# Two GNN layers on one core: PSUM banks shared by all uses, results taken seven chunks after their products

## The chip, the core and the metric

The kernel runs on one core of one Trainium2 chip. The metric is the device time of a run in microseconds (us). Three runs of the kernel before gave 1674.48, 1678.09 and 1674.82 us.

## What is computed

A graph network of two GIN layers, then a residual and a layer norm, all in float32. There are 6250 nodes with 256 features and 100000 edges, sorted by destination. Low-numbered nodes have many more edges than high-numbered ones.

```python
def agg(h, eps): return (1 + eps) * h + segment_sum(h[src], dst, 6250)
h = agg(x, eps1)                       # 6250 x 256
h = relu(h @ W1a + b1a)                # 256 -> 512
h = relu(h @ W1b + b1b)                # 512 -> 512
h = agg(h, eps2)                       # 6250 x 512
h = relu(h @ W2a + b2a)                # 512 -> 512
out = layernorm(x + (h @ W2b + b2b))   # 512 -> 256, no scale or shift
```

## The kernel before

The nodes are 49 tiles of 128 rows, and the edges 782 chunks of 128. Both layers run the same function, `layer`, which writes out the order of every engine's work by hand: a Python loop issues instructions, and each engine executes its own in that order.

**Edges that are counted.** The destinations of the first 216 chunks all lie in the four "heavy" tiles 0 to 3. For these, layer 1 makes a table of how often each source meets each destination (`counting`): per step DVE makes two one-hot tables (ca, cb; `make`), TensorE multiplies them into PSUM (pc, L775), ACT copies the result (cs, L766), DVE adds it to the table at (L750). The table, converted to float32 and multiplied with the features (`products`: pm<-xr,cf, L683; 13 ranges of four source tiles for each of four heavy tiles), gives the sums of the heavy tiles; DVE adds each of the 52 results to the accumulator acc (L689). Layer 1 stores the table in HBM (counts, SP queue, L759) and layer 2 loads it from there (L696).

**Edges that are gathered.** The other 566 chunks are 94 groups of 20 down to 4 chunks (63 have 4). GpSimd issues an indirect DMA for each chunk (`gather`, L264) that brings the 128 source rows into a ring of 24 chunks: 6 pieces of 4, each refilled when TensorE has used it. Layer 1 keeps the ring in early; layer 2, whose rows are twice as wide, in early and late. In the main loop each piece of four chunks is summed by TensorE against one-hot tables sel (pm, L887, 32 columns a chunk, four chunks beside each other). When a group is complete, ACT copies the sum (split<-pm, L906), TensorE moves its rows to their places (pu<-split,to, L911), and DVE adds it to the accumulators of the three or four tiles it may belong to, under a mask (L915). DVE makes sel and to of the group after next right after a group (`select`, L552, L557).

**Dense layers.** Accumulators are held for blocks of four tiles, at most four blocks at a time (ACCS). `seed` loads a block's own rows into acc (SP queue, L535), and five chunks later ACT multiplies them by 1 + eps (L542), for which it waits until they have landed. When all groups and products of a block are added, `block` runs the two dense layers: transposes (pt, L611; copied by ACT to zt, L614), first matrix (ph, L623; ACT's relu to ht, L627), second matrix (po, L634), then `finish` (layer 1: DVE add, ACT relu, store of h on ACT's queue; layer 2: DVE adds and statistics, and in `conclude2` the norm and the store on SP's queue, L991).

**The order.** Three things are woven together in the main loop. After each chunk, `now` goes up by one, `due` issues what was put off with `later`, and two queues are pumped: blockwise (the dense layers, a credit of up to 4.0 us) and beside (counting and products), at a rate that `spread` plans. Each step yields its planned TensorE cost. Of the blocks only the first in the queue advances.

**PSUM.** There are eight banks of 512 float32 columns. In layer 1 three hold sums (pm, pu and products; `sum_tile`), three the dense results (mm) and two the counts (pc); in layer 2 five hold sums and three dense results. A sum is taken LAG = 2 chunks after it was asked for, or when its bank is needed; pu follows split by one chunk. Dense results are copied right after their product (zt, ht), or one chunk after (`finish`).

## Time and profile before

| | |
|---|---|
| median of three runs | 1674.82 us |
| the profiled execution, its own time | 2010.4 us |
| its span, first to last instruction | 2008.7 us |
| mean granted TensorE clock | 0.853 |
| busy: TensorE, DVE, ACT, GpSimd | 1405.2, 822.3, 371.4, 1087.8 us |
| idle time of GpSimd that a wait for pm (L887) ended, both layers | 309.4 us |
| adds of products to acc (L689) | 104, 57.7 us |

The profile is of one execution, which was longer than the three runs. In a group of instructions the page gives busy time, the mean of one and the idle time before them with what ended it. "Remote", and in the chain of waits "another core or an unknown queue", means that the profile shows no event that ended a wait. Each float32 matmul has two records.

### The profile page before, as it was taken

What the parts mean: (1) busy time and instruction counts of PE and PEld (TensorE: products, weight loads), DVE (VectorE), ACT (ScalarE), POOL (GpSimd) and SP (SyncE); (2) the same over time, 40 slices, a digit from 0 to 9 for tenths busy, and PEclk for the clock granted to TensorE, in tenths of its full rate; (3) what the DMA queues carried; (4) which work ended last, traced back from release to release, by engine and by line L of the source; (5) the groups of instructions that cost most, each with busy time, mean ns of one, the idle gap of its engine ahead of it and who ended that gap; (6) DMA issues with size and microseconds to landing.
All of it is one profiled execution on the core that took longest, in us unless ns stands there. A gap on an engine that the chain in (4) does not pass through costs nothing.

```text
span 2008.7 us, 17209 instructions
## 1 busy us (share of the span) xinstructions
PE 1405.2 (70%) x5364; PEld 617.0 (31%) x5364; DVE 822.3 (41%) x2256; ACT 371.4 (18%) x683; POOL 1087.8 (54%) x1147
## 2 busy tenths in 40 slices
PE   1344757674867887978656858695869768878877
PEld 0111223332433444423312223241323323324334
DVE  4665453534344434333111213332425355456543
ACT  0222232321322222212100001111101111112111
POOL 5666665656556556451276755656555464455520
PEclk9766787787878988988878879797979889989989
DMA  5433354546436557331487766757676475565631
GB/s 150 139 92 92 97 176 144 169 144 180 149 119 205 172 174 224 116 110 48 175 290 241 242 203 212 228 178 234 192 234 199 126 261 161 154 193 173 180 102 38
DMA packets 157811, 337.08 MB, mean 168 GB/s; under 512 B 23954, under 2 KB 70930, under 8 KB 157712
## 3 DMA queue, kind: packets, MB, share of 16 engines
q0 software_dynamic: 72448, 222.63, 37.0%
q1 hardware_dynamic: 74756, 96.90, 14.4%
q10 hardware_dynamic: 10508, 16.35, 2.3%
q8 instruction: 47, 0.77, 0.2%
q14 instruction: 52, 0.43, 0.1%
HBM read 303.75 MB, written 32.05 MB: 167 GB/s over the span
## 4 chain that ended last, share of the span: by engine, by line
PE 41%; issue 18%; another core or an unknown queue 15%; DVE 11%; DMA 6%; POOL 4%; ACT 3%; SPq 1%; DVEq 0%; ACTq 0%; POOLq 0%
PE ph L623 12%; PE po L634 10%; PE pm L683 8%; PE pm L887 5%; PE pu L911 4%; POOL early L264 3%; DVE acc L915 3%; DMA acc<-h 2%; DVE at L750 1%; PE pc L775 1%; PE pt L611 1%; ACT split L906 1%; ACT zt L614 1%; DVE cb L736 1%
## 5 line engine op out<-in xcount | busy, mean ns | idle before, releaser
L264 POOL DMA_INDIRECT early<-in_x_dram,srcs x566 | 547.0, 967 | 366.4 <-issue 149.2
L264 POOL DMA_INDIRECT early<-h,srcs x288 | 274.1, 952 | 267.9 <-PE pm L887 84.2
L915 DVE SCALAR_TENSOR_TENSOR acc<-pu,mask,acc 128x256 f32<-128x256 f32 (+1 forms) x666 | 365.2, 608 | 105.6 <-PE ph L623 22.9
L264 POOL DMA_INDIRECT late<-h,srcs x278 | 263.4, 948 | 210.6 <-PE pm L887 109.4
L683 PE MATMUL pm<-xr,cf 128*128 128x256 f32 (+3 forms) x784 | 311.0, 545 | 44.8 <-issue 21.1
L911 PE MATMUL pu<-split,to 128*128 128x256 f32 (+2 forms) x376 | 186.8, 583 | 206.1 <-ACT split L906 136.8
L689 DVE TENSOR_TENSOR acc<-pm,acc 128x256 f32<-128x256 f32 (+1 forms) x104 | 57.7, 556 | 415.5 <-remote 162.5
L683 PEld LDWEIGHTS pm<-xr,cf 128*128 128x128 f32 (+1 forms) x784 | 165.4, 218 | 202.5 <-issue 152.0
L887 PE MATMUL pm<-early,sel 128*32 128x256 f32 (+1 forms) x1708 | 191.4, 527 | 49.6 <-issue 16.5
L623 PE MATMUL ph<-zt,w2a_s 128*128 128x512 f32 (+1 forms) x416 | 184.9, 596 | 27.8 <-ACT zt L614 27.7
L775 PE MATMUL pc<-cb,ca 128*128 128x490 f16 x216 | 87.7, 475 | 141.5 <-issue 41.6
L634 PE MATMUL po<-w1b_s,ht 128*128 128x512 f32 (+1 forms) x392 | 175.5, 599 | 0.0
L911 PEld LDWEIGHTS pu<-split,to 128*128 128x128 f32 (+1 forms) x376 | 70.6, 215 | 304.6 <-ACT split L906 174.4
L906 ACT COPY split<-pm 128x256 f32<-128x256 f32 (+2 forms) x188 | 88.0, 479 | 362.6 <-remote 164.6
L766 ACT CAST cs<-pc 128x490 f16<-128x490 f32 x151 | 84.0, 570 | 199.7 <-remote 115.6
L623 PEld LDWEIGHTS ph<-zt,w2a_s 128*128 128x128 f32 x416 | 78.5, 199 | 136.6 <-issue 89.5
L552 DVE TENSOR_TENSOR sel<-iota,slot 128x128 f32<-128x128 f32 (+5 forms) x188 | 65.4, 348 | 124.0 <-remote 96.7
L623 PE MATMUL ph<-zt,w1a_s 128*128 128x512 f32 (+1 forms) x208 | 102.3, 629 | 7.7 <-issue 5.1
L887 PE MATMUL pm<-late,sel 128*32 128x512 f32 x556 | 90.0, 647 | 18.1 <-issue 14.4
L557 DVE TENSOR_SCALAR to<-iota,home 128x128 f32<-128x128 f32 x188 | 57.4, 305 | 109.5 <-PE pu L911 66.9
L634 PEld LDWEIGHTS po<-w1b_s,ht 128*128 128x128 f32 (+1 forms) x392 | 74.1, 191 | 89.0 <-issue 87.1
L614 ACT COPY zt<-pt 128x256 f32<-128x256 f32 (+2 forms) x98 | 44.7, 483 | 284.1 <-remote 209.3
(111 smaller groups left out, 941.2 us busy)
## 6 DMA issues: line engine op xcount, KB each, us to landing
xr<-in_x_dram SPq DMA_DIRECT2D x48, 512.0 KB
h<-h1r ACTq DMA_DIRECT2D x48, 256.0 KB
counts<-cf SPq DMA_DIRECT2D x48, 256.0 KB
acc<-h SPq DMA_DIRECT2D x12, 1024.0 KB
xr<-h SPq DMA_DIRECT2D x12, 1024.0 KB
cf<-counts SPq DMA_DIRECT2D x48, 256.0 KB
early<-in_x_dram,srcs POOLq DMA_INDIRECT x566
acc<-in_x_dram SPq DMA_DIRECT2D x12, 512.0 KB
```

The lines of the kernel that those rows point to most:

```text
L264: nc.gpsimd.indirect_dma_start(out=rows_[:, j, :], out_offset=None, in_=table, in_offset=bass.IndirectOffsetOnAxis(ap=srcs[:, c : c + 1], ...
L552: nc.vector.tensor_tensor(sel[:, :n, :], iota[:, :SLOTS].unsqueeze(1).to_broadcast([P, n, SLOTS]), slot[:, c0 : c0 + n].unsqueeze(2).to_br ...
L614: nc.scalar.copy(zt[:, :, i * P : i * P + m], pt[:, :, :m])
L623: nc.tensor.matmul(ph[:, :nb], wa[:, k, f * P : (f + 1) * P], zt[:, k, :nb], start=(k == 0), stop=(k == kk - 1),)
L634: nc.tensor.matmul(po[:m], ht[:, f, i * P : i * P + m], wb[:, f, :], start=(f == 0), stop=(f == KH - 1),)
L683: nc.tensor.matmul(pm, cf[:m, j, :], xr[:m, j, :], start=(j == 0), stop=(j == len(ks) - 1),)
L766: nc.scalar.copy(cs, pc)
L775: mm = nc.tensor.matmul(pc, a, b, start=(i == 0), stop=(i == len(pair) - 1))
L887: mm = nc.tensor.matmul(pm[b * SLOTS : (b + 1) * SLOTS], sel[:, c - c0, :], rows_[:, j, :], start=(c == parts[b][0]), stop=(c == parts[b][ ...
L906: nc.scalar.copy(split[:used], pm[:used])
L911: nc.tensor.matmul(pu, to[:used], split[:used], start=True, stop=True)
L915: nc.vector.scalar_tensor_tensor(acc[t], pu, mask[:, t - lo[g], g : g + 1], acc[t], op0=ALU.mult, op1=ALU.add,)
```

## The change

`sum_tile`, `take` and the three PSUM pools go. Each layer holds eight bank tiles, in 16 halves, and `place(n)` gives a half (up to 256 columns) or a whole bank to any use: pm, pu, products, pc, pt, ph, po. Halves whose neighbour is in use go first. While an accumulation of several matmuls is open, nothing else is put in its bank. When nothing is free, the result that is due first is taken at once. LAG is 7 for all of them, and now for zt, ht, `finish` and cs too; pu follows split by two chunks, and the add to the table follows cs by two.

A block counts its results that are still to be taken (pending), and yields None while there are any; the blockwise queue has two hands and then lets the next block take a step. In layer 1 the 13 products of a heavy tile stay open in one bank (`once`) and are added once. The products of a heavy tile start when its counts have been added. The order of `select` moves: half a group later, for groups of over 4 chunks. There are more buffers for sel of small groups (4), to (6), split (3) and cs (4). Set-up tables that only the preparation uses are moved to its pool; the clearing of dsti goes from GpSimd to DVE. The core of the diff, with removed lines left out from `later` on:

```diff
@@ -27,7 +27,10 @@
 STEP1 = 1.1
 STEP2 = 1.5
 ACCS = 4
-LAG = 2
+LAG = 7
+BLOCKS = 2
+BANKS = 8
+BANK = 512
 SPREAD = 5.0
 TILES = 4
 SIGMAS = 6.5
...
@@ -504,9 +507,12 @@
             edge = ctx.enter_context(tc.tile_pool(name=f"edge{number}", bufs=3))
             dense = ctx.enter_context(tc.tile_pool(name=f"dense{number}", bufs=2))
             psum = ctx.enter_context(
-                tc.tile_pool(name=f"psum{number}", bufs=2, space=bass.MemoryType.PSUM)
+                tc.tile_pool(name=f"psum{number}", bufs=1, space=bass.MemoryType.PSUM)
             )
-            SUMS = 3 if number == 1 else 5
+            banks = [
+                psum.tile([P, BANK], F32, tag=f"bank{i}", name=f"bank{i}") for i in range(BANKS)
+            ]
+            halves = [(i, j) for i in range(BANKS) for j in range(2)]
             acc = {}
             held = []
...
             def seed(ts):
                 while len(held) >= ACCS:
+                    if not blockwise.todo:
+                        due(all=True)
                     assert blockwise.todo
                     blockwise.step()
+                    tick()
                 held.append(ts)
                 a = edge.tile([P, TILES, width], F32, tag="acc", name="acc", bufs=ACCS)
...
@@ -562,39 +578,70 @@
             delayed = []
             now = 0
...
+            def later(chunks, what, frees=False):
+                delayed.append((now + chunks, what, frees))
+            def undelay(item):
+                delayed.remove(item)
+                item[1]()
             def due(all=False):
                 while delayed:
                     item = min(delayed, key=lambda d: d[0])
                     if not all and item[0] > now:
                         break
...
+                    undelay(item)
                 for b in list(waiting):
                     if not any(uses[t] or left[t] for t in b):
                         blockwise.todo.append(block(b))
                         waiting.remove(b)
...
+            def tick():
+                nonlocal now
+                now += 1
+                due()
+            opened = []
+            def place(n, whole=False):
+                while True:
+                    here = [h for h in halves if h[0] not in opened]
+                    single = [h for h in here if (h[0], 1 - h[1]) not in halves]
+                    double = [h for h in here if (h[0], 1 - h[1]) in halves]
+                    if 2 * n <= BANK and (single or double):
+                        i, j = (single or double)[0]
+                        mine = [(i, j)]
+                        break
+                    if 2 * n > BANK and double:
+                        i = next(h[0] for k, h in enumerate(double) if (h[0], 1 - h[1]) in double[:k])
+                        j = 0
+                        mine = [(i, 0), (i, 1)]
+                        break
+                    undelay(min((d for d in delayed if d[2]), key=lambda d: d[0]))
+                for h in mine:
+                    halves.remove(h)
+                if not whole:
+                    opened.append(i)
+                return banks[i][:, j * BANK // 2 : j * BANK // 2 + n], mine
+            def complete(p):
+                opened.remove(p[1][0][0])
+            def free(p):
+                halves.extend(p[1])
+            def take_later(p, what):
+                def take():
+                    what(p[0])
+                    free(p)
+                later(LAG, take, frees=True)
@@ -602,44 +649,66 @@
                 nb = sum(rows(t) for t in ts)
                 early = prepare(dense, ts)
+                pending = 0
+                def result(p, what):
+                    nonlocal pending
+                    def taken():
+                        nonlocal pending
+                        pending -= 1
+                    def take(ap):
+                        what(ap)
+                        later(1, taken)
+                    pending += 1
+                    take_later(p, take)
                 zt = dense.tile([P, kk, TILES * P], F32, tag="zt", name="zt")
                 for i, t in enumerate(ts):
                     m = rows(t)
...
+                    pt = place(kk * P, whole=True)
                     a = acc.pop(t)
                     for k in range(kk):
                         nc.tensor.transpose(
...
+                            pt[0][:, k * P : k * P + m], a[:m, k * P : (k + 1) * P], ident[:m, :m]
                         )
...
+                    result(pt, lambda ap, i=i, m=m: nc.scalar.copy(
+                        zt[:, :, i * P : i * P + m],
+                        ap.rearrange("p (k j) -> p k j", j=P)[:, :, :m],
+                    ))
                     if t == ts[-1]:
                         held.remove(ts)
                     yield 0.11 * kk
...
+                while pending:
+                    yield None
                 ht = dense.tile([P, KH, TILES * P], F32, tag="ht", name="ht")
                 for f in range(KH):
...
+                    ph = place(TILES * P, whole=True)
                     for k in range(kk):
                         nc.tensor.matmul(
...
+                            ph[0][:, :nb], wa[:, k, f * P : (f + 1) * P], zt[:, k, :nb],
                             start=(k == 0), stop=(k == kk - 1),
                         )
...
+                    result(ph, lambda ap, f=f: nc.scalar.activation(
+                        ht[:, f, :nb], ap[:, :nb], AF.Relu, bias=ba[:, f : f + 1]
+                    ))
                     yield 0.00167 * kk * nb
...
+                while pending:
+                    yield None
                 for i, t in enumerate(ts):
                     m = rows(t)
...
+                    po = place(wide, whole=True)
                     for f in range(KH):
                         nc.tensor.matmul(
...
+                            po[0][:m], ht[:, f, i * P : i * P + m], wb[:, f, :],
                             start=(f == 0), stop=(f == KH - 1),
                         )
...
+                    result(po, lambda ap, t=t, m=m, i=i: finish(dense, t, m, ap, i, early))
                     yield 0.00167 * KH * wide
...
+                while pending:
+                    yield None
                 yield from conclude(dense, ts, early)
             def products(turns, table_of):
@@ -676,20 +745,24 @@
                         load(i + 1)
                     xr, cf = factors.pop(0)
                     ks = ranges[r]
...
+                    opens = not once or r == 0
+                    closes = not once or r == len(ranges) - 1
+                    if opens:
+                        pm = place(width)
                     for j, k in enumerate(ks):
...
+                            pm[0], cf[:m, j, :], xr[:m, j, :],
+                            start=(opens and j == 0), stop=(closes and j == len(ks) - 1),
                         )
...
+                    def add_product(ap, t=t):
+                        nc.vector.tensor_tensor(acc[t], ap, acc[t], op=ALU.add)
                         left[t] -= 1
...
+                    if closes:
+                        complete(pm)
+                        take_later(pm, add_product)
                     yield 0.00167 * len(ks) * width
             def load_counts(cf, r, ks, t):
...
@@ -760,29 +833,30 @@
                         counts[r, t, :, : n * P], cf[:, :n, :].rearrange("p k j -> p (k j)")
                     )
...
                 def step():
                     c, pair, made = ready.pop(0)
...
+                    pc = place(NT * W, whole=True)
                     for i, (a, b) in enumerate(pair):
                         mm = nc.tensor.matmul(
...
+                            pc[0], a, b, start=(i == 0), stop=(i == len(pair) - 1)
                         )
                         if i == 0:
                             together(mm, [made])
...
+                    def copy(ap, c=c):
+                        cs = edge.tile([P, NT * W], F16, tag="cs", name="cs", bufs=4)
+                        nc.scalar.copy(cs, ap)
+                        later(2, lambda: add(c, cs))
+                    take_later(pc, copy)
                     if todo:
                         make(*todo.pop(0))
                     return STEP1 if len(pair) == 1 else STEP2
+                def products_of(t):
+                    while added <= end[t]:
+                        yield 0.0
+                    yield from products([(r, t) for r in range(len(ranges))], convert)
                 total = len(todo)
                 make(*todo.pop(0))
...
@@ -796,39 +870,40 @@
                 for t in heavy:
                     n = end[t] + 1 - steps
+                    d = min(LAG + 3, n // 2)
                     for i in range(n):
                         steps += 1
                         yield step()
...
+                        if i >= d:
+                            k = len(ranges) + 1
+                            for _ in range((i + 1 - d) * k // (n - d) - (i - d) * k // (n - d)):
+                                yield next(product, 0.0)
                     yield from product
...
+                    product = products_of(t)
                 yield from product
...
             class Queue:
...
+                def __init__(self, rate, hands=1):
                     self.rate = rate
                     self.credit = 0.0
                     self.todo = []
+                    self.hands = hands
+                    self.over = []
                 def step(self):
...
+                    for w in self.todo[: self.hands]:
+                        if w not in self.over:
+                            cost = next(w, self)
+                            if cost is self:
+                                self.over.append(w)
+                            elif cost is not None:
+                                self.credit -= cost
+                                break
+                    while self.todo and self.todo[0] in self.over:
+                        self.over.remove(self.todo.pop(0))
                 def pump(self):
                     self.credit = min(self.credit + self.rate, 4.0)
...
@@ -844,7 +919,7 @@
             due(all=True)
             select(order[0])
             select(order[1])
...
@@ -893,44 +967,44 @@
                     last_sum[upto] = mm
                     gathered[upto + PIECES] = gather(upto + PIECES, table, width, *places)
                     for c, b in pieces[upto][1]:
...
+                        tick()
                         for q in both:
                             q.pump()
                     upto += 1
...
+                def add_group(ap, g=g, to=to, parts=parts):
+                    split = edge.tile([P, width], F32, tag="split", name="split", bufs=3)
                     used = SLOTS * sum(1 for p in parts if p)
...
+                    nc.scalar.copy(split[:used], ap[:used])
+                    def add(ap):
+                        for t in range(lo[g], min(hi[g], NT - 1) + 1):
+                            nc.vector.scalar_tensor_tensor(
+                                acc[t], ap, mask[:, t - lo[g], g : g + 1], acc[t],
+                                op0=ALU.mult, op1=ALU.add,
+                            )
+                            uses[t] -= 1
                     def unite():
...
+                        pu = place(width, whole=True)
+                        nc.tensor.matmul(
+                            pu[0], to[:used], split[:used], start=True, stop=True
+                        )
+                        take_later(pu, add)
+                    later(2, unite)
+                complete(pm)
+                take_later(pm, add_group)
                 if k + 2 < len(order):
...
+                    n = len(members[order[k + 1]])
+                    later(n // 2 if n > PARTS else 0, lambda k=k: select(order[k + 2]))
             due(all=True)
             blockwise.todo += [block(b) for b in waiting]
             while blockwise.todo:
                 blockwise.step()
...
+                tick()
             due(all=True)
         def prepare1(dense, ts):
```

## The prediction, made before the changed kernel was run

> **What bounds the kernel now.** I read the page first, then the busy time by stage, then the timeline across one long stall, then TensorE's waits.
>
> ```profile
> PE 1405.2 (70%) x5364; PEld 617.0 (31%) x5364; DVE 822.3 (41%) x2256; ACT 371.4 (18%) x683; POOL 1087.8 (54%) x1147
> ...
> PE 41%; issue 18%; another core or an unknown queue 15%; DVE 11%; DMA 6%; POOL 4%; ACT 3%; SPq 1%; DVEq 0%; ACTq 0%; POOLq 0%
> ...
> L264 POOL DMA_INDIRECT early<-in_x_dram,srcs x566 | 547.0, 967 | 366.4 <-issue 149.2
> ```
>
> No engine is full. The chain that ended last spends 15% of 2008.7 us, 307 us, on a releaser that the profile can't name. I cut the span where the gathers of each layer begin to follow TensorE and where they end:
>
> ```profile
> core 0: us, PE busy (x) PEld busy (x) DVE busy (x) ACT busy (x) POOL busy (x), PEclk, DMA share, GB/s
> 0.00:54.00 54.00, 10.81 (x46) 5.44 (x50) 26.77 (x216) 0.00 (x0) 27.27 (x40) 1.00 0.49 148
> 54.00:917.00 863.00, 582.59 (x2445) 272.64 (x2438) 387.09 (x1174) 217.55 (x431) 522.67 (x542) 0.82 0.48 146
> 917.00:987.00 70.00, 53.31 (x167) 23.61 (x165) 16.70 (x39) 16.41 (x31) 0.79 (x2) 0.92 0.15 52
> 987.00:1933.00 946.00, 699.70 (x2481) 283.39 (x2482) 358.95 (x749) 124.23 (x195) 536.72 (x566) 0.87 0.66 208
> 1933.00:2009.00 76.00, 58.78 (x236) 31.95 (x234) 32.76 (x80) 13.23 (x27) 0.31 (x1) 0.96 0.10 32
> ```
>
> The columns are microseconds with counts in brackets, then the granted clock. The two long stages hold 1809 of 2009 us. TensorE is idle in 26 to 32% of them, and its clock is down to 0.82 and 0.87. Now one stall in layer 2:
>
> ```profile
> 1042.80 1.18 PE L887 MATMUL pm<-late,sel 128*32 128x512 f32 x8 [2.34 <-DMA late<-h,srcs]
> ...
> 1058.95 0.94 POOL L264 DMA_INDIRECT early<-h,srcs  x1 [0.30 <-issue]
> 1063.61 0.58 ACT L906 COPY split<-pm 128x512 f32<-128x512 f32 x1 [40.91 <-remote]
> 1063.61 0.69 DVE L552 TENSOR_TENSOR sel<-iota,slot 128x512 f32<-128x512 f32 x1 [18.22 <-remote]
> 1063.85 1.27 POOL L264 DMA_INDIRECT early<-h,srcs  x1 [3.96 <-remote]
> ```
>
> All engines stand still while GpSimd works off its gathers, 1.25 us apart, and all start together. The chain's unnamed part is 18.8% of the layer 1 stage (162 us) and 15.2% of the layer 2 stage (144 us).
>
> ```profile
> PE pu L911 <- ACT split L906: 136.8, 42, 20.3
> ...
> PE pc L775 <- ACT cs L766: 33.9, 10, 14.6
> ...
> PE ph L623 <- ACT zt L614: 30.3, 7, 15.0
> PE pc L775 <- DVE ca L732: 29.4, 11, 6.8
> ...
> PE pt L611 <- ACT zt L614: 27.6, 4, 7.8
> ```
>
> These are microseconds, times and the longest. They are the waits the change can reach: TensorE waits for a PSUM result to be copied (split, zt, cs) before it uses the copy or the bank.
>
> **The profiled time and the median.** The profiled execution took 2010.4 us (span 2008.7), the shown runs 1674.82 in the median: 336 less. The unnamed 307 us nearly close that gap (2010 - 307 = 1703), so I take them to belong to the profiled execution and count them neither as a gain nor as a loss. Without them the stages are 54 + 701 + 70 + 802 + 76 = 1703, which is 28 above the median.
>
> [...] clock 0.65 in 100-200 us with TensorE 46% busy, 0.97 in 1800-1900 us at 91%. [...] So I use the spacing of gathers, not their record of 0.95 us.
>
> **The floor.** Gathers that don't wait are 1.25 us apart (1057.69, 1058.95 and so on; 0.95 of record and 0.30 of issue). Layer 1 needs 542 x 1.25 = 678 us in its stage, layer 2 566 x 1.25 = 708. TensorE's own work at full clock, from undisturbed runs of the chain (0.429 us a 512-wide record, half for 256, 3.06 us for 24 gather records): in layer 2, ph 416 x 0.429 = 178, products 392 x 0.429 = 168, pm 1132 x 0.1275 = 144, po 392 x 0.216 = 85, pu 188 x 0.429 = 81, pt about 22: 678 us. In layer 1 the same sum is about 511 (po 168, ph 89, products 84, pm 74, pc 45, pu 40, pt 11). So GpSimd's spacing is the floor in both: room is 701 - 678 = 23 us in layer 1 and 802 - 708 = 94 in layer 2, 117 in all. Less the 28 that the median already lacks: **89 us of room**, floor 1675 - 89 = 1586.
>
> **The change, part by part.**
> 1. LAG 2 to 7, unite 1 to 2 chunks. A copy or add now enters the ACT or DVE queue about 7 x 1.25 = 8.8 us after its product rather than 2.5, and pu waits two chunks for split. Nothing is added to run; work is moved later in two queues. What it removes: pu for split 136.8, pc for cs 33.9. Much of that lies inside the unnamed stalls (20.28 us of it in the one shown), so it isn't all a gain.
> 2. Eight shared banks. Without them LAG 7 would run out. Demand in layer 2, a group of 4 chunks: pm (4 + 7)/4 = 2.75, pu 7/4 = 1.75, products 52 x 7/566 = 0.64, a block of 12 results each 40 chunks or so 12 x 7/40 = 2.1: 7.2 of 8. When none is free the oldest result is taken early; the real lag then is some 4 to 6 chunks. Cost between 0 and 1 us a time; I take 0, because that result is ready by then.
> 3. Two blocks at a time; a phase waits for its copies by letting other work pass. Removes ph for zt 30.3 and pt for zt 27.6 (again partly inside stalls). A block now takes about 12 steps and three pauses of 8 chunks, 36 chunks, just within the 36 to 40 at which blocks come, so no extra block is left for the end. If one were, about 22 us would follow a layer's last gather. I take 0. What moves with a result moves whole: in layer 1 the DVE add, ACT's relu and the store of h on ACT's queue; in layer 2 four DVE instructions, and by the longer pauses the store of the output, which sits on SP's queue ahead of later counts and seed loads. That queue waited 386 us for the output's rows already (L991), while nobody waited much for counts (11.2 us), so I price the move at 0 to 10 us and take 0.
> 4. Layer 1's products stay open over 13 ranges: 52 adds of about 0.42 us become 4. That is 20 us less on DVE, which is 45% busy there: 0 on the path.
> 5. sel is issued up to half a group later, with 4 buffers for small groups: bound -3 to +3 us; I take 0.
> 6. The seeds' loads and the ACT scale behind them (ACT acc for DMA acc<-h, 71.9 us in 7 waits, longest 30.4) stay. ACT still stops there; what is queued behind it is split and zt. TensorE now has 9 us of slack before it needs them. Accumulators are held 11 chunks longer; by the schedule at most four are held, so seeds keep their lead.
> 7. Set-up memsets moved; dsti's 0.75 us goes from POOL to DVE: under 1 us, hidden by loads.
>
> **What is late next** is the gather. TensorE must keep 1.25 us a chunk; at full clock layer 2 asks 678/566 = 1.20. At a clock of 0.94 they are equal, and it has 0.87 now. Hence not all of the room: of the 89 I take layer 1's share whole (23 x 89/117 = 17) and two thirds of layer 2's 72, 48: 65. **Forecast 1675 - 65 = 1610 us**, its own range 1588 to 1640.
>
> **Rivals.**
> - *The gather spacing isn't the floor in unprofiled runs.* For it: TensorE nearly never waits for gathers (7.9 + 2.3 + 5.2 us). Against: the spacing is so constant. Then the gain is the named waits outside the unnamed stalls: the TensorE waits of both stages that parts 1 to 3 reach sum to 299 us; the unnamed 307 of 526 us idle are 58%, leaving 42%, 126: **1549**.
> - *Slower: halves of one bank serialise.* In layer 1 pm, pu and pt take halves, and a half whose neighbour is unread is preferred. If a read must wait for the newest write beside it, and TensorE for the read, each of 188 results costs a round trip: pm's end to pu through split was about 1.2 us (at 1022). TensorE's 583 busy us reach 701 with 98 of these; that is where it decides. With three quarters (141 x 1.2 = 169) layer 1 is at 752, 51 worse; with 20 gained in layer 2, **1706**. Against: pieces of 4 chunks are written at once, and the oldest free half is taken first.
> - *Little:* the waits go over to the acc<-h loads and to SP's queue, which the change leaves; only 5 to 10 us are won: **1668**.
>
> **Chances.** Forecast 0.60; gathers not the floor 0.14; little 0.13; slower 0.13. About 0.2% is what a measurement can tell from no change here. Faster 0.60 + 0.14 + 0.08 = 0.82, same 0.05, slower 0.13. The range holds the forecast's case, most of the first rival's and of the third: 1545 to 1670.
>
> **What would show it.** Right: pu for split, pc for cs, ph and pt for zt nearly gone; clock over 0.9 in both long stages; gathers that wait for pm (115.8 us in layer 1, 193.6 in layer 2) at a third; TensorE waiting for gathers instead; adds at L689 from 104 to 56. Wrong: split, zt or adds in layer 1 waiting for pm matmuls of another group (the second rival); or the stages after the last gathers (70 and 76 us) growing by 20, which would refute part 3; or a layer 2 stage under 700 us, which would refute the floor.

## The result and the profile after

| | before | after |
|---|---|---|
| median of four runs each | 1676.45 us (1674.48 to 1690.22) | 1635.57 us (1631.62 to 1638.67) |
| ratio | | 0.9738, 95% interval 0.9681 to 0.9795 |
| the execution that the page shows, its time and span | 2010.4, 2008.7 us | 1631.6, 1629.9 us |

The forecast was 1610 us, with a range of 1545 to 1670. The change gains 41 us where 65 were forecast.

One thing must be known to read the numbers: on some of the chips (called disturbed below) the kernel before takes 2000 to 2008 us, with stalls that have no named end, and on the others 1675 to 1678. The first profile of before comes from a disturbed chip and that of after doesn't, so the comparison below uses another trace of before, span 1677.1 us (the first experiment).

From the page of the changed kernel: engines, the chain that ended last, one row of gathers.

```profile
PE 1342.9 (82%) x5364; PEld 602.7 (37%) x5364; DVE 807.6 (50%) x2209; ACT 366.3 (22%) x683; POOL 1092.9 (67%) x1146
...
PE 51%; POOL 15%; DMA 13%; DVE 10%; issue 9%; ACT 1%; DVEq 0%; ACTq 0%; SPq 0%; POOLq 0%
...
L239 POOL DMA_INDIRECT early<-in_x_dram,srcs x566 | 550.5, 973 | 182.3 <-issue 152.7
```

Nothing in the chain is without a name. GpSimd, on which the prediction set the floor, has 15% of it, and DMAs, mostly gathers that TensorE waits for, 13%. Of the 182.3 us in which GpSimd stood idle ahead of layer 1's gathers, 152.7 are "issue", the 0.3 us that stand ahead of every gather in this trace (at least 303 ns, 305 in the median), also of one that waits for nothing.

The busy time by stage, cut as before at the first gather that follows TensorE and at the last gather of each layer (columns as in the prediction). The stage behind a layer's last gather, the third and the fifth row, is called its tail:

```profile
0.00:40.00 40.00, 10.55 (x42) 5.28 (x46) 27.82 (x215) 0.00 (x0) 26.08 (x38) 1.00 0.66 190
40.00:736.00 696.00, 548.01 (x2407) 257.94 (x2400) 364.84 (x1113) 207.28 (x419) 526.91 (x542) 0.86 0.59 180
736.00:818.00 82.00, 64.60 (x204) 30.16 (x202) 23.75 (x54) 22.32 (x44) 0.05 (x1) 0.91 0.17 59
818.00:1544.00 726.00, 652.40 (x2472) 270.35 (x2472) 353.88 (x744) 121.90 (x193) 539.61 (x566) 0.95 0.83 270
1544.00:1630.00 86.00, 67.32 (x248) 38.93 (x244) 37.29 (x87) 14.78 (x29) 0.26 (x1) 0.91 0.13 40
```

The waits of the changed kernel: engine, line, releaser, then us in all, times, longest. L960 is pm, L991 pu, L979 split, L690 ph, L677 zt.

```profile
PE bank L960 <- DMA early<-in_x_dram,srcs: 96.9, 45, 4.0
...
PE bank L960 <- DMA early<-h,srcs: 24.0, 8, 6.3
PE bank L960 <- DMA late<-h,srcs: 20.8, 9, 5.4
...
POOL early L239 <- PE bank L960: 15.8, 19, 4.4
...
POOL late L239 <- PE bank L960: 11.0, 9, 7.2
...
PE bank L991 <- ACT split L979: 9.9, 6, 3.0
...
PE bank L690 <- ACT zt L677: 8.0, 7, 3.6
```

TensorE's largest waits are for gathers, 141.7 us together. GpSimd waits for TensorE (pm) only 26.8 us, and TensorE for split 9.9.

### The profile page after: what moved, and what is told of

Same layout as the page of the kernel before. It is cut to its first block, busy times and chain, and to the rows that moved or that the text cites. A ratio compares the mean times of both kernels' runs of the same rounds, so it can differ in the third digit from the quotient of the medians.

```text
span 1629.9 us, 17159 instructions
## 1 busy us (share of the span) xinstructions
PE 1342.9 (82%) x5364; PEld 602.7 (37%) x5364; DVE 807.6 (50%) x2209; ACT 366.3 (22%) x683; POOL 1092.9 (67%) x1146
## 4 chain that ended last, share of the span: by engine, by line
PE 51%; POOL 15%; DMA 13%; DVE 10%; issue 9%; ACT 1%; DVEq 0%; ACTq 0%; SPq 0%; POOLq 0%
PE bank L704 15%; PE bank L690 15%; POOL early L239 13%; PE bank L754 7%; PE bank L960 7%; PE bank L991 5%; DMA early<-in_x_dram,srcs 4%; DVE acc L983 3%; DMA late<-h,srcs 3%; DMA early<-h,srcs 3%; POOL late L239 2%; PE bank L674 1%; DMA h<-h1r 1%; DVE at L866 1%; DVE r L1057 1%
## 5 line engine op out<-in xcount | busy, mean ns | idle before, releaser
L239 POOL DMA_INDIRECT early<-in_x_dram,srcs x566 | 550.5, 973 | 182.3 <-issue 152.7
L983 DVE SCALAR_TENSOR_TENSOR acc<-bank,mask,acc 128x256 f32<-128x256 f32 (+1 forms) x666 | 365.6, 608 | 322.7 <-PE bank L991 209.4
L754 PE MATMUL bank<-xr,cf 128*128 128x256 f32 (+3 forms) x784 | 294.0, 521 | 24.9 <-issue 19.2
L960 PE MATMUL bank<-early,sel 128*32 128x256 f32 (+1 forms) x1708 | 187.9, 518 | 148.0 <-DMA early<-in_x_dram,srcs 96.9
L754 PEld LDWEIGHTS bank<-xr,cf 128*128 128x128 f32 (+1 forms) x784 | 158.1, 205 | 158.7 <-issue 136.9
L991 PE MATMUL bank<-split,to 128*128 128x256 f32 (+2 forms) x376 | 183.6, 573 | 16.3 <-ACT split L979 9.9
L690 PE MATMUL bank<-zt,w2a_s 128*128 128x512 f32 (+1 forms) x416 | 178.8, 586 | 4.2 <-ACT zt L677 4.2
L979 ACT COPY split<-bank 128x256 f32<-128x256 f32 (+2 forms) x188 | 89.3, 481 | 384.8 <-PE bank L960 282.3
L704 PE MATMUL bank<-w1b_s,ht 128*128 128x512 f32 (+1 forms) x392 | 173.5, 595 | 0.4 <-ACT cs L848 0.4
L960 PEld LDWEIGHTS bank<-early,sel 128*32 128x32 f32 x1708 | 39.2, 115 | 269.3 <-issue 190.4
L760 DVE TENSOR_TENSOR acc<-bank,acc 128x512 f32<-128x512 f32 (+1 forms) x56 | 37.4, 668 | 165.5 <-PE bank L754 143.0
L690 PEld LDWEIGHTS bank<-zt,w2a_s 128*128 128x128 f32 x416 | 79.4, 200 | 100.5 <-issue 94.8
L991 PEld LDWEIGHTS bank<-split,to 128*128 128x128 f32 (+1 forms) x376 | 62.0, 203 | 137.3 <-issue 79.1
L690 PE MATMUL bank<-zt,w1a_s 128*128 128x512 f32 (+1 forms) x208 | 99.1, 619 | 3.8 <-ACT zt L677 3.8
L960 PE MATMUL bank<-late,sel 128*32 128x512 f32 x556 | 75.8, 619 | 29.4 <-DMA late<-h,srcs 20.8
L704 PE MATMUL bank<-w2b_s,ht 128*128 128x256 f32 (+1 forms) x392 | 89.0, 380 | 0.0
```

Of the source, the lines that this page charges most:

```text
L239: nc.gpsimd.indirect_dma_start(out=rows_[:, j, :], out_offset=None, in_=table, in_offset=bass.IndirectOffsetOnAxis(ap=srcs[:, c : c + 1], ...
L690: nc.tensor.matmul(ph[0][:, :nb], wa[:, k, f * P : (f + 1) * P], zt[:, k, :nb], start=(k == 0), stop=(k == kk - 1),)
L704: nc.tensor.matmul(po[0][:m], ht[:, f, i * P : i * P + m], wb[:, f, :], start=(f == 0), stop=(f == KH - 1),)
L754: nc.tensor.matmul(pm[0], cf[:m, j, :], xr[:m, j, :], start=(opens and j == 0), stop=(closes and j == len(ks) - 1),)
L760: nc.vector.tensor_tensor(acc[t], ap, acc[t], op=ALU.add)
L960: mm = nc.tensor.matmul(pm[0][b * SLOTS : (b + 1) * SLOTS], sel[:, c - c0, :], rows_[:, j, :], start=(c == parts[b][0]), stop=(c == parts[ ...
```

## The experiments

### The kernel before, where nothing disturbs it

The kernel before, unchanged, ran twice more, first on a disturbed chip.

> The kernel before, unchanged, for a second profile. Theory (gather pace): the unnamed 307 us belonged to the first profiled execution; a profile of about 1675 us shows the two gather stages at 720 to 750 and 770 to 790 us against 1.25 us x 542 and 566 = 678 and 708, GpSimd waiting 60 to 110 us for pm, and 60 to 80 us after each layer's last gather. Rival (the stalls are the kernel's own): about 2010 us again, with some 300 us of unnamed waits in the chain.

It took 2005.03 us (the runs beside it 2008.27 in the median), with waits whose end has no name as in the first profile (ACT's split 203.6 us in 18 of them, the longest 40.6). So the unnamed time isn't a matter of one execution: on that chip all eleven runs beside it took as long (1997.63 to 2024.43 us). The second time:

> The kernel before again, for a trace that isn't disturbed. If this chip is undisturbed: a span near 1675 us, nothing without a name in the chain. Theory of the prediction (taking the unnamed 307 us out of the first trace): stages of 54, 701, 70, 802 and 76 us, so gather spacings about 23 us over the floor in layer 1 and 94 in layer 2, with TensorE waiting for split, zt and cs. Rival (the stalls stood also in place of other waits, so the split between the layers is different): the two long stages sum to about 1475 us again, but layer 1 is 30 us or more off 701. If the chip is disturbed: about 2008 us, and nothing new.

It took 1678.78 us. Its stages and the waits that matter here:

```profile
0.00:41.00 41.00, 10.22 (x39) 5.05 (x43) 26.09 (x213) 0.00 (x0) 26.61 (x40) 1.00 0.63 187
41.00:755.00 714.00, 562.54 (x2461) 264.48 (x2454) 389.42 (x1176) 217.32 (x433) 525.54 (x541) 0.87 0.58 177
755.00:814.00 59.00, 44.83 (x155) 20.02 (x153) 16.70 (x39) 15.46 (x29) 1.46 (x3) 0.95 0.19 63
814.00:1601.00 787.00, 671.89 (x2480) 274.09 (x2481) 358.21 (x751) 123.64 (x195) 537.10 (x566) 0.92 0.77 250
1601.00:1677.00 76.00, 59.42 (x238) 32.33 (x236) 32.51 (x80) 13.20 (x26) 0.66 (x1) 0.96 0.11 33
```

```profile
PE pm L887 <- DMA early<-in_x_dram,srcs: 84.7, 40, 5.2
...
POOL early L264 <- PE pm L887: 76.9, 30, 9.2
...
PE pu L911 <- ACT split L906: 62.9, 38, 12.6
...
POOL late L264 <- PE pm L887: 40.1, 15, 6.8
...
PE pm L887 <- DMA late<-h,srcs: 19.1, 5, 5.5
...
PE pm L887 <- DMA early<-h,srcs: 12.5, 4, 5.3
...
PE pc L775 <- ACT cs L766: 10.9, 8, 5.9
...
PE ph L623 <- ACT zt L614: 5.3, 4, 2.1
```

The theory's layer 1 stage, 701, was 714; its layer 2 stage, 802, was 787: as the two stages sum to 1501 and not 1475, and layer 1 is 13 off and not 30, the rival is out. The waits are smaller than in the first profile: pu for split 62.9 and not 136.8, and ph for zt, 30.3 there, is 5.3 here. One wait is larger: TensorE waits for gathers 84.7 + 19.1 + 12.5 = 116.3 us, and hardly did in the first profile.

The changed kernel ran again too:

> The changed kernel itself, on the chip of this set. Theory (its time is the spacing of gathers, 542 x 1.25 + 566 x 1.25 = 1386 us, plus about 250 us at the start and behind the last gathers): 1632 to 1640 us where the chip is undisturbed, 0.974 of the kernel before. On a chip that takes 2008 us for the kernel before, the stalls without a named releaser come on top: about 1870 us there, as the variant with the last group drawn forward took, with gather spacings about 0.07 us over 1.25 in the mean. Rival (the unnamed stalls are something that only the kernel before has): 1635 us on either chip.

It took 1633.5 us beside 1677.93 for the kernel before, ratio 0.9748 (0.9722 to 0.9775); that chip was undisturbed, so what theory and rival say of the other kind of chip stays untried.

Stage by stage, after less before: start -1, layer 1 gathers **-18**, tail **+23**, layer 2 gathers **-61**, tail **+10**; sum -47, which is 1629.9 - 1677.1. Layer 1 as a whole gained nothing (773 to 778 us); layer 2 gained 51 (863 to 812). In the trace of the second run of the changed kernel the tails were 83 and 89 us.

Where the gathers come late can be read from their start times. Before, the intervals of 1.3 us or more exceed 1.25 us by 118.6 us in both layers together, and 101.8 of these lie in each layer's last 252 gathers, which belong to the groups of four chunks. Of the changed kernel's 34.1 us, 22.0 lie there. So the change pays where groups are small, and the copies and adds that each group brings come most often.

### The delay alone, in the shared banks

```diff
-LAG = 7
+LAG = 2
```

> The changed kernel with LAG 2 in place of 7, everything else kept (shared banks, two blocks, products of layer 1 closed once). Theory: the late taking is what lets TensorE keep the gathers' pace, so most of the gain goes back: 1655 to 1680 us, GpSimd waits for pm of 50 us or more. Rival (it is the second block, or the adds and clears that went away): 1630 to 1640 us, as the changed kernel.

On the disturbed chip: 1981.51 us against 2008.27, ratio 0.9864 (0.979 to 0.994). The times expected were for the other kind of chip. It ran again on one of those:

> The changed kernel with the delay set back from seven chunks to two; shared banks, two blocks at a time and the open products stay. On the disturbed chip this took 0.986 of the kernel before. Theory (the delay is the part that pays, the shared banks are what makes it possible): 0.99 to 1.01 of the kernel before on an undisturbed chip, TensorE waiting for split by 100 us or more, tails of 72 and 81 us. Rival (banks and blocks pay by themselves, the delay is a small part): 0.975 to 0.985.

Undisturbed: 1674.4 us against 1674.86, ratio **0.9994** (0.9981 to 1.0007). Its waits and the four last stages:

```profile
PE bank L991 <- ACT split L979: 61.8, 36, 10.4
```

```profile
40.00:751.00 711.00, 563.15 (x2442) 264.40 (x2434) 372.65 (x1125) 217.96 (x429) 523.36 (x541) 0.86 0.57 178
751.00:821.00 70.00, 56.14 (x180) 24.95 (x176) 18.64 (x43) 17.76 (x34) 1.07 (x2) 0.94 0.15 53
821.00:1598.00 777.00, 674.61 (x2487) 273.92 (x2487) 360.68 (x756) 124.81 (x196) 536.79 (x565) 0.93 0.78 253
1598.00:1673.00 75.00, 60.45 (x230) 32.48 (x230) 29.50 (x73) 12.81 (x26) 0.95 (x1) 0.95 0.11 35
```

At a delay of two, shared banks, two blocks and open products together gain nothing that can be told from zero. The wait for split is as long as before the change (61.8 against 62.9, and not the 100 expected). Going on to seven takes 15 us out of the layer 1 stage and 51 out of layer 2's, and adds 12 and 11 to the tails. The delay is that of all results at once; which of them needs it is told by the waits alone, where split's fell from 61.8 to 9.9.

### The delay without the shared banks

The kernel before with

```diff
-LAG = 2
+LAG = 7
-                to = edge.tile([P, P], F32, tag="to", name="to")
+                to = edge.tile([P, P], F32, tag="to", name="to", bufs=5)
```

> The kernel before with the delay of two chunks raised to seven, in its own separate PSUM pools (and five buffers instead of three for the small table of a group's slots). Theory (the delay pays only if there are banks enough: three banks for group sums and three for the dense layers run out, and then the oldest result is taken at once): half or less of the change's gain, ratio 0.985 to 1.0. Rival (the delay is all of it, banks don't matter): 0.974, as the whole change. Second rival (a queue of copies held later in front of full pools stops TensorE more): over 1.0.

1735.57 us against 1677.93, ratio **1.0367** (1.0331 to 1.0404): slower, the second rival. In this kernel LAG holds for the sums alone (pm, pu, products); zt, ht, cs and `finish` are taken as before, and pu follows split by one chunk. It tries the longer delay in the old pools, not all of the change but the banks.

```profile
PE pu L911 <- ACT split L906: 59.4, 27, 13.6
PE pm L887 <- DVE acc L915: 27.6, 15, 3.4
PE pm L887 <- ACT split L906: 18.8, 9, 3.9
...
PE pu L911 <- DVE acc L915: 13.2, 11, 2.1
```

By the code, with three or five banks for sums `sum_tile` finds none free, takes the oldest result at that moment, and the product that needs the bank comes right behind the copy or the add. pm now waits for DVE's adds 27.6 us (2.5 before) and for split 18.8 (not among the 20 largest waits before), while pu still waits 59.4 for split. So neither the delay nor the banks, with what goes with each here, gain anything alone; in one kernel they gain 41.

### One block at a time

```diff
-BLOCKS = 2
+BLOCKS = 1
```

> The changed kernel with one block in the dense layers at a time. Theory: a block then needs some 36 chunks for its pauses and cannot keep up with one block each 36 to 40, so blocks pile up and are worked off behind the last gathers; the stages of gathers stay at 696 and 726 us, the two tails of 83 and 87 us grow by 10 to 40 us each: 1650 to 1700 us on an undisturbed chip, ratio to the kernel before 0.985 to 1.015. Rival (one block keeps up, two at a time buy nothing): the same time as the changed kernel within 0.5%.

1655.42 us, ratio to before 0.9864 (0.9837 to 0.989); in the same set the changed kernel has 1633.5, so one block costs 22 us.

```profile
40.00:731.00 691.00, 539.76 (x2416) 253.86 (x2409) 372.61 (x1136) 205.85 (x419) 526.10 (x542) 0.85 0.59 182
731.00:822.00 91.00, 74.73 (x203) 35.24 (x201) 16.78 (x32) 23.54 (x43) 0.63 (x1) 0.94 0.15 52
822.00:1536.00 714.00, 633.66 (x2396) 258.52 (x2396) 346.51 (x724) 119.19 (x187) 538.17 (x566) 0.94 0.83 272
1536.00:1654.00 118.00, 95.10 (x320) 53.20 (x320) 43.75 (x106) 17.81 (x34) 0.87 (x1) 0.88 0.12 39
```

The tails are 9 and 32 us longer than in the changed kernel, TensorE's busy time in them 10 and 28. In layer 2 one whole block more is left behind, as the theory had it: 32 more records of ph and 32 of po, which is what a block of four tiles has, 24.2 us. In layer 1 most of one is. But the stages of gathers became 5 and 12 us **shorter**, not the same: TensorE's work that is left behind isn't in them (539.76 us and not 548.01, 633.66 and not 652.40). Layer 2's, at 714, is within 8 us of the 565 intervals of 1.25 us.

### Why the tails grew

The records of ph (L623 before, L690 after) in the tails tell what stands there. First layer 1, before and after, then layer 2 after and with one block at a time (columns: us of the stage, TensorE, its weight loads, clock, DMA share, GB/s):

```profile
755.00:814.00 59.00, 9.17 (x32) 4.82 (x32) 0.95 0.19 63
736.00:818.00 82.00, 19.25 (x48) 9.37 (x48) 0.91 0.17 59
1544.00:1630.00 86.00, 35.76 (x96) 18.50 (x96) 0.91 0.13 40
1536.00:1654.00 118.00, 52.74 (x128) 25.41 (x128) 0.88 0.12 39
```

A layer 1 block has 16 records of ph. So the changed kernel leaves the first product of one more block behind layer 1's last gather; in layer 2 it is 96 records against 88 before.

Two attempts to shorten the tails. The first lets the last group pass before the queues are emptied, and empties both behind it (core):

```diff
-                if k == len(order) - 1:
-                    while any(q.todo for q in both):
...
-            blockwise.todo += [block(b) for b in waiting]
-            while blockwise.todo:
-                blockwise.step()
-                tick()
+            while any(q.todo for q in both) or delayed or waiting:
+                for q in both:
+                    q.step()
+                    tick()
```

> The changed kernel without the loop that empties both queues ahead of the last group: the last group's sum, split and unite are issued at once, and the rest of the dense blocks follows, so tile 48's block doesn't come after everything. Theory (the growth of the two tails is the last group's chain standing alone at the end): 15 to 25 us less, 1612 to 1622, tails of 83 and 87 us down to 70 to 75. Rival (the tails are the longer pauses in the blocks, or TensorE work that is left over): within 5 us of 1635.

It ran on the disturbed chip: 1871.12 us against 2008.27, ratio 0.9308 (0.9258 to 0.9357). Its tails:

```profile
867.00:944.00 77.00, 61.95 (x205) 28.38 (x203) 24.01 (x56) 22.40 (x44) 0.70 (x2) 0.94 0.18 64
1785.00:1870.00 85.00, 69.72 (x252) 37.72 (x248) 40.05 (x95) 16.62 (x33) 0.61 (x1) 0.88 0.13 41
```

TensorE is busy for 61.95 and 69.72 us in them, where the changed kernel has 64.60 and 67.32. About as much work is still behind the last gather, so the order of emptying isn't what puts it there. Whether the 5 us in layer 1 are real can't be told across chips.

The second cuts the delay near the end of each layer (with `lag = LAG` set at its start, and used in `take_later`):

```diff
+                if k == len(order) - 12:
+                    lag = 2
```

> The changed kernel with the delay cut from seven chunks to two for results taken from the twelfth group before the end of each layer on; everything else stays. Theory (the two tails of 83 and 87 us are longer than the 70 and 76 of the kernel before because at a delay of seven the block ahead of the last still has its transposes and much of its first products to do when the last gather has gone): tails of 70 to 76 and 76 to 82 us, 15 to 24 us less in all, stages of gathers as they were or up to 5 us longer: 1615 to 1625 us, ratio 0.963 to 0.969. Rival (the tails are long because of the order in which the last group and the blocks are emptied, not because of the delay): no change, 1632 to 1640 us. Second rival (a short delay in front of the end brings the waits for split back, and the gathers slow down there): 1640 us or more.

1635.0 us, ratio 0.9748 (0.9723 to 0.9774), as the changed kernel: no gain, the time that the first rival expected.

```profile
40.00:742.00 702.00, 548.00 (x2410) 259.78 (x2402) 369.90 (x1118) 209.52 (x422) 524.95 (x541) 0.86 0.57 180
742.00:827.00 85.00, 64.92 (x196) 28.93 (x196) 20.07 (x47) 20.39 (x40) 1.23 (x3) 0.84 0.13 46
827.00:1560.00 733.00, 657.19 (x2471) 272.79 (x2472) 357.27 (x748) 123.30 (x194) 537.90 (x566) 0.94 0.82 267
1560.00:1640.00 80.00, 64.74 (x246) 34.19 (x244) 33.38 (x82) 13.80 (x27) 0.61 (x1) 0.94 0.12 41
```

Layer 2's tail fell by 6 us, but its stage grew by 7; layer 1's tail didn't shorten, and 48 records of ph stand in it as before. The gathers slow down near the end: layer 1's last 24 took 42.6 us and not 34.3, layer 2's last 72 took 112.1 and not 104.7. (The profiled execution was the longest of its five, 1641.6 us, so a few us of each row are its own.) My theory named the right kind of work, a block that comes late, and a cure that doesn't work. The rival's cause, the order of emptying, was out already. What makes the block late isn't shown beyond this.

### A quarter of the gathers left out

```diff
-            for j, (c, b) in enumerate(pieces[i][1])
+            for j, (c, b) in enumerate(pieces[i][1]) if i < PIECES or j < 3
```

In the kernel before:

> The kernel before with every fourth gather left out after the first six pieces (the matmuls run on whatever the buffer holds, so the sums are not the reference's). Theory (the kernel before is paced in layer 1 by its own waits, in layer 2 by waits and a slow clock, and has only some 110 us of gather spacing to give): on an undisturbed chip 40 to 90 us less than the kernel before, mostly out of layer 2; on a disturbed one 250 or more less, because the stalls go with the gathers in flight. Rival (gathers pace the kernel before as they pace the changed one): 270 to 300 us less on an undisturbed chip, a quarter of 1108 x 1.25 = 346 us less what turns up behind it.

1561.99 us against 1677.93 (0.9314, 0.9289 to 0.9339), 116 less.

```profile
41.00:667.00 626.00, 531.30 (x2446) 249.82 (x2442) 384.70 (x1177) 216.26 (x431) 399.11 (x406) 0.93 0.57 174
667.00:736.00 69.00, 51.36 (x176) 22.88 (x170) 16.71 (x39) 17.07 (x32) 1.20 (x2) 0.94 0.19 63
736.00:1474.00 738.00, 655.12 (x2474) 269.25 (x2475) 357.88 (x749) 122.95 (x194) 408.35 (x430) 0.95 0.67 218
```

It lies between the two expectations, and against mine in its place: 88 us come out of the layer 1 stage and 49 out of layer 2's, where the 135 intervals left out of each, at 1.25 us, are 169. So another limit stands close behind the gathers. In layer 1 the gathers paced the kernel already before the change, and TensorE ran there at a clock of 0.93 with a quarter of them gone, against 0.87.

In the changed kernel, twice, both times on a disturbed chip:

> The changed kernel with one of four gathers left out after the first 24 chunks of each layer (the matmuls read the old rows, so the sums are others): 430 or so in place of 566 a layer. Theory (GpSimd's 1.25 us a gather is the floor): layer 1's stage falls from 696 to 570 to 600 us, layer 2's from 726 to about 680 to 700, where TensorE's 678 us at full clock take over; 1470 to 1510 us in all. Rival (TensorE and its waits set the pace): 1600 to 1635 us.

> The changed kernel with every fourth gather left out after the first six pieces, again (the sums are not the reference's); the first time it stood on the disturbed chip, where it took 1625 us. The same cut took the kernel before from 1678 to 1562 us on an undisturbed chip. Theory (the spacing of gathers is what sets the two long stages of the changed kernel; with a quarter of them gone TensorE's 1344 busy us are next, about 84% busy as in the cut kernel before, or more): 1500 to 1560 us, both stages 60 us or more shorter. Rival (gathers and TensorE are late together in the changed kernel, so cutting gathers alone buys little; the 1625 us were no disturbance): 1590 to 1625 us, TensorE then waiting for something other than gathers. If the cut changed kernel is slower than the cut kernel before (1562), the change costs TensorE something that the gathers had covered.

1624.7 us against 2008.27, and 1630.68 against 2000.57 (0.8134, 0.809 to 0.8177). Both times lie far over the theory (1470 to 1510, 1500 to 1560) and in or just over the rival's range (1600 to 1635, 1590 to 1625), but on a kind of chip for which the ranges weren't worked out. The unnamed time is 4% of the chain in both, against 10% in the variant with the last group drawn forward, which has all its gathers. TensorE is busy 83% of the span, and the gathers wait for pm, 213.9 and 57.8 us in the first of the two runs. How far the changed kernel would come down with fewer gathers where nothing disturbs it wasn't seen, so the rival, that gathers and TensorE are late together in it, stays open.

## Why the prediction was right, and where it missed

- **The unnamed 307 us are no part of the gain.** Right in effect: undisturbed, before has 1677 us and nothing unnamed. That they belong to the profiled execution was wrong: the second trace on such a chip has them too, and the eleven runs beside it took 1997.63 to 2024.43 us. The stages cleaned of them (54, 701, 70, 802, 76) were 41, 714, 59, 787, 76, so what was over stood in the start (13), a tail (11) and layer 2 (15), less 13 that layer 1's stage lacked.
- **The floor is the gathers' spacing.** Right as a lower bound that the changed kernel comes close to; that nothing else stands as close isn't shown for it (the runs with fewer gathers leave that open). From the start times of the gathers, I sum by how much intervals of 1.3 us or more exceed 1.25 us. Before: 37.7 us in layer 1, 80.9 in layer 2. After: 16.9 and 17.2. The 541 and 565 intervals take 695.1 and 725.2 us, where 1.25 us each would be 676 and 706.
- **Room taken: 17 us in layer 1 and 48 in layer 2.** Measured 18 and 61. The caution about a clock of 0.94 was too great, for a reason in its sum: the 678 us for layer 2 count TensorE's whole work, also what runs behind the last gather (59.4 us before). Within the stage it is about 672 x 0.92 = 618 us at full clock before and 652 x 0.95 = 620 after, an estimate, so 1.1 us a chunk and not 1.20, and the clock at which the two are equal is about 0.88. Before had 0.92 already, after has 0.95, and TensorE idles 74 us of its stage (726 - 652) instead of 115 (787 - 672). Layer 1's clock didn't reach 0.9 (0.87 to 0.86). That the clock would go up as TensorE is kept busier was the author's estimate, from two stretches of the first trace; measured by stage, TensorE was busy for 79% of layer 1's stage before and after, and in layer 2 for 85% at 0.92 and 90% at 0.95.
- **Part 1, the delay.** Right that it removes the wait of pu for split (62.9 to 9.9) and of pc for cs (10.9 to none). That GpSimd's waits for pm go to a third or less was right as well: 117.0 to 26.8. The delay at seven is worth 39 to 41 us against a delay of two (1635.57 and 1633.5 us against 1674.4).
- **Part 2, shared banks at no cost.** No cost was found: DVE's masked add takes 608 ns in both kernels, split's copy 479 and 481 ns. The slower rival, halves of a bank that serialise, is out: it was the author's conjecture, which no trace of before showed, and its 1.2 us were an estimate from one place (at 1022 us TensorE's weight loads stood idle for 1.10 us until split was copied). The prediction said that the delay would run out of banks without them; the delay of the sums in the old pools was in fact 58 us slower.
- **Part 3, two blocks: the step that failed.** "No extra block is left for the end. If one were, about 22 us would follow a layer's last gather. I take 0." The tails grew by 23 and 10 us, 33 in all, against the undisturbed kernel before. The text had named a growth of 20 us as what would refute the part; layer 1's tail passes it against the undisturbed 59 us, not against the 70 that the text started from. TensorE's busy time behind the last gather went from 44.8 to 64.6 us in layer 1, where the first product of one more block stands there, and from 59.4 to 67.3 in layer 2. Twelve of the 23, and all of the 10, come with the delay of seven (tails of 70 and 75 at two, 82 and 86 at seven); the other eleven come with the rest of the change, and which part of it isn't settled (at a delay of two, 44 records of ph stand behind layer 1's last gather, 12 of the 16 that came); nor is how the delay does its share, as a short one near the end doesn't take it back in layer 1. The price of a block was nearly right: the one more that stands behind layer 2's last gather with one block at a time has 24.2 us. (That one block at a time costs 22 us in all is another figure: tails 9 and 32 longer, stages 5 and 12 shorter.) What two blocks remove isn't ph's wait for zt, which was 5.3 us before and is 8.0 after, but a block that at this delay would be left over.
- **Part 4, open products.** The adds fell from 104 records of 57.7 us to 56 of 37.4, 20 us less, as said. That it is 0 on the path is only as sure as the delay-of-two variant, in which it stands together with other parts: within 0.2% of zero.
- **Parts 5 to 7** weren't tried by themselves; the same bound holds for them, and like that of part 4 it was measured at a delay of two.

In sum: -17 - 48 + 0 = -65 was forecast; -18 - 61 + 33 - 1 = -47 was measured in the traces, 41 in the medians (the trace of before is 4 us over the median of its set, that of after is the fastest of its four). The tails are the miss, and layer 2's larger gain covers part of it: that two errors of opposite sign meet is luck. The gain of layer 1's stage isn't one: TensorE's busy time there fell by 14.5 us, and 19.8 more of it stand behind the last gather.

The rivals: that the spacing isn't the floor (1549) is out by the spacings, and what spoke for it, that TensorE nearly never waits for gathers, held in the disturbed trace only (116.3 us in the other); "little" (1668) and "slower" (1706) are out by the ratio.

## What to carry to other kernels

Here a longer delay between a product and its use paid only with enough places for the results that wait, so count both together (the places with a delay of two: 0; the delay of the sums in the old pools: +58 us; both in one kernel: -41). When one stream paces a stage, price the end separately: here a longer delay (seven against two: stages 15 and 51 us shorter, tails 12 and 11 longer) and a queue that works its blocks more slowly (one block at a time: stages 5 and 12 us shorter, tails 9 and 32 longer) made the stage shorter and put work behind it, so add stage and tail before calling it a gain. When a profile has much time without a name and the runs shown are far shorter, take a trace elsewhere before reading waits from it: the wait for split was half of what the first profile gave (62.9 and 136.8 us), and that for zt a sixth (5.3 and 30.3).

## What the runs showed of the hardware

The same program took 1675 to 1678 us in the median on some chips and 2000 to 2008 on others, and the runs of before in a set of 11 to 27 lay within 2% of each other (1997.63 to 2024.43 us, 1669.65 to 1681.36, 1669.61 to 1683.64, 1984.54 to 2019.87). In the trace on a disturbed one there are stalls that only GpSimd works through: in the one that the prediction shows, ACT waited 40.9 us and DVE 18.2, while GpSimd issued gathers 1.25 us apart, and the engines started together 3.7 us after the last of them. The changed kernel, with the last group drawn forward, loses about 240 us there (1871 against about 1635 for the changed kernel on the other chips), the kernel before 330 (2008.27 against 1677.93), and the changed kernel with a quarter of its gathers left out takes 1625 to 1631 there. What sets these chips apart, and why the engines stand still there, is not settled; a shorter ring of gathers wasn't tried.

Gathers with no more than that 0.3 us of idle time ahead start 1.25 us apart in the median, in both layers (1251 ns in the first trace of before, 1254 in that of the changed kernel), although a row of layer 2 is twice as wide as one of layer 1 (512 features and 256).
